# Grouping the activations of the gate, pointwise and feed-forward products by tile, with the side work held meanwhile

## The chip, the cores and the metric

The kernel runs on one core of one Trainium2 chip. The metric is device time in microseconds (us) of one execution; the kernel before is given as the median of three runs. TensorE is PE in the profile (its weight loads are PEld), VectorE is DVE, ScalarE is ACT, GpSimd is POOL and SyncE, which issues most of the DMAs, is SP.

## The reference

Two layers, all in float32, on an image batch of 4 x 64 x 64 positions with 256 channels.

```python
# layer 0, a block with a selective scan
xz = layernorm(x) @ in_proj_W                      # 256 -> 2 x 384
x_proj, z = split(xz)
y_ssm = 0.5 * (scan_fwd(windows(x_proj)) + scan_bwd(...))   # 2x2 windows, 8 states, dt = silu(...)
y_dw = depthwise_3x3(x_proj)
y_conv = gelu(y_dw @ pw_W)
y = (alpha * y_ssm + (1 - alpha) * y_conv) * silu(z) @ out_W
x1 = x + y
x1 = x1 + gelu(layernorm(x1) @ fuse_W1 + fuse_b1) @ fuse_W2 + fuse_b2   # 256 -> 512 -> 256
# layer 1, self-attention of each image over its 4096 positions
f, g, h = x1 @ Wf + bf, x1 @ Wg + bg, x1 @ Wh + bh  # 32, 32 and 256 channels
out = gamma * (softmax(g @ f.T) @ h @ Wo + bo) + x1
```

## The kernel before

Layer 0 is cut into 32 tiles of 512 positions (8 image rows; 8 tiles to an image, `NBLK` = 8). Layer 1 takes 128 queries at a time against 32 chunks of 128 keys; the last ones, when layer 0 is done, are taken 256 at a time by other functions (`late_weights`, `attend_late`).

The source is a set of Python generators. Each yields an estimated cost after every small piece of work, and the order in which the generators are advanced is the order in which instructions are written down. A scheduler then orders them for each engine, earlier written first where both are ready. What sets the written order:

- `scan(at)` is the chain of a tile. A step forms decays on ACT (`decays`, Exp, L406), transposes them on PE into a PSUM bank (`turned`, L462), and multiplies and adds on DVE (`decayed` L470 and L474, `carried` L492, `given` L485).
- Beside it run the side pieces of the tile before and of the next one: `conv` (the depthwise taps, on DVE from the second image on, L595), `gate` (three products with `win`, L342, each followed by a Silu, L346), `tail` (three pointwise products, L626, each with two Gelus, L631; the output product, L649; a layer norm; four feed-forward products, L669, each with a Gelu, L673; the second feed-forward product, L680; the inputs of layer 1) and `next_head` (layer norm and first product of a coming tile, L327). `weave` advances two of them in proportion to their costs. `first_layer` gives the side pieces 1.2 cost units for each unit of the scan (`SHARE`).
- `prepare(at)` makes what the next tile's scan needs, the steps `dt` among it (six products L382, six Silus L389), at the end of the scan before.
- From the second image on, layer 1 is the outer loop: `attend` writes eight steps of four value products (L1039) for 128 queries, and behind each step calls `fill(5.7)`, which advances layer 0 by 5.7 cost units (`RATE`). `weights` makes the scores (L844, copied out of PSUM by ACT in L852), their maxima (DVE, L860) and the exponentials (L877, L878) of the next queries.

PSUM has eight banks. Three are for the scan (`bank`), one is for the value products, and four (`q0` to `q3`) are handed out in turn by `aside()` to every side product; `four()` takes all four for a set of scores.

ACT holds one set of function tables at a time. Exp, Silu and Gelu are in different sets, so that a change from one to another puts an ACT_TABLE_LOAD before the instruction, whose time the profile puts down to that instruction's line. Copies and the Identity function need no load. For the tiles of the first image `gate` is already written as one run (`whole`); for the others each of its three products is a piece of its own:

```python
nc.scalar.activation(zs[:, f, :], pz, AF.Silu, bias=b_in[:, KI + f : KI + f + 1])
if not whole:
    yield 1.72
```

Of the kernel before, what the change touches and what calls it, by code (L numbers as in the profile page):

```python
# [31 lines left out]
NST = 8  # L32
# [27 lines left out]
def block_then_attention_kernel(  # L60
# [111 lines left out]
        return ins  # L172

    turn = [0]

    def aside(shape=(P, TOK)):

# [158 lines left out]
    def gate(at, whole):  # L336
        xnT = heads[at][0]
        zs = one.tile([P, KI, TOK], F32, tag="zs", name="zs")
        for f in range(KI):
            pz = aside()  # L340
            for k in range(KD):
                nc.tensor.matmul(  # L342
                    pz, lhsT=win[:, k, INNER + f * P : INNER + (f + 1) * P], rhs=xnT[:, k, :],
                    start=(k == 0), stop=(k == KD - 1),
                )
            nc.scalar.activation(zs[:, f, :], pz, AF.Silu, bias=b_in[:, KI + f : KI + f + 1])  # L346
            if not whole:
                yield 1.72
        gates[at] = zs
        if whole:  # L350
            yield 5.2

    def prepare(at):

        _, xc = heads[at]

        pj = aside()
        for k in range(KI):
            nc.tensor.matmul(pj, lhsT=wx[:, k, :], rhs=xc[:, k, :], start=(k == 0), stop=(k == KI - 1))
        proj = one.tile([P, TOK], F32, tag="proj", name="proj")  # L360
        nc.scalar.copy(proj, pj)
        yield 2.58
        pbc = aside((P, 4, 2, 64))
        for t in range(4):
            nc.tensor.transpose(pbc[:, t].rearrange("p d e -> p (d e)"), proj[:, t * P : (t + 1) * P], ident)
        bc = two.tile([P, 4, 2, 2 * NST], F32, tag="bc", name="bc")
        nc.vector.tensor_copy(bc, pbc[:, :, :, RANK:])
        cbn = st.tile([P, 8, NST], F32, tag="cbn", name="cbn")
        bc8 = bc.rearrange("p t d e -> p (t d) e")
        nc.vector.tensor_tensor(cbn, bc8[:, :, :NST], bc8[:, :, NST:], ALU.mult)  # L370
        cb = st.tile([P, 8], F32, tag="cb", name="cb")
        nc.vector.tensor_reduce(cb, cbn, AX.X, ALU.add)
        yield 1.1
        dts = [two.tile([P, KI, TOK], F32, tag="dt", name="dt") for _ in range(2)]
        for f in range(KI):
            pds = [aside() for _ in range(2)]

            with tc.high_priority():
                last = None
                for d in range(2):  # L380
                    last = behind(
                        nc.tensor.matmul(  # L382
                            pds[d], lhsT=wdt[64 * d : 64 * d + RANK, f * P : (f + 1) * P],
                            rhs=proj[64 * d : 64 * d + RANK, :], start=True, stop=True,
                        ),
                        last,
                    )
            for d in range(2):
                nc.scalar.activation(  # L389
                    dts[d][:, f, :], pds[d], AF.Silu, bias=v("dt_b_b" if d else "dt_b_f", f)  # L390
                )
            if at >= NBLK:
                yield 1.1
        steps[at] = bc, cb, dts, {}
        if at < NBLK:
            yield 3.3
            if at > 0:
                yield from gate(at - 1, True)
        decays(at, 0, 0)

    def decays(at, n, d):
# [25 lines left out]
    def scan(at, ensue):  # L427
# [69 lines left out]
        pas = {(0, 0): turned(0, 0)}  # L497
        for j in range(3 * NST + 1):
            n, k = divmod(j, 3)
            first, second = j < 3 * NST, j > 0  # L500
            if k == 2 and n + 1 < NST:
                decays(at, n + 1, 1)
            if first and k == 1 and n + 1 < NST:
                decays(at, n + 1, 0)
            p0 = decayed(0, j, pas.pop((0, j))) if first else None
            p1 = decayed(1, j - 1, pas.pop((1, j - 1))) if second else None
            if first:
                carried(0, j, p0)
                if j + 1 < 3 * NST:
                    pas[0, j + 1] = turned(0, j + 1)  # L510
                pas[1, j] = turned(1, j)
                yield 1.3
            if second:
                carried(1, j - 1, p1)
            if first:
                given(0, j, p0)
            if second:
                given(1, j - 1, p1)
            yield 2.0
            if j == 3 * NST - 4:  # L520
                ensue = ensue()
            if j >= 3 * NST - 4:
                for cost in ensue:
                    yield cost
                    if j < 3 * NST and cost > 2.0:
                        break
# [88 lines left out]
    def tail(at):  # L615
# [4 lines left out]
        load_rows(xo, at)  # L620

        yz = one.tile([P, KI, TOK], F32, tag="yz", name="yz")
        for f in range(KI):
            pw = aside()
            for k in range(KI):
                nc.tensor.matmul(  # L626
                    pw, lhsT=wpw[:, k, f * P : (f + 1) * P], rhs=ydw[:, k, :],
                    start=(k == 0), stop=(k == KI - 1),
                )
            for t2 in range(2):  # L630
                nc.scalar.activation(  # L631
                    yz[:, f, t2 * 256 : (t2 + 1) * 256].rearrange("p (t1 wr wc) -> p t1 wr wc", t1=2, wr=ROWS // 2),
                    pw.rearrange("p (wr t2 wc t1) -> p t2 t1 wr wc", wr=ROWS // 2, t2=2, t1=2)[:, t2],
                    AF.Gelu,
                )
            yield 2.58

        for f in range(KI):
            nc.vector.scalar_tensor_tensor(
# [23 lines left out]
        if at + 3 < LAST:  # L663
            load_head(at + 3)
        ff = one.tile([P, KF, TOK], F32, tag="ff", name="ff")
        for f in range(KF):
            pf = aside()
            for k in range(KD):
                nc.tensor.matmul(  # L669
                    pf, lhsT=wf1[:, k, f * P : (f + 1) * P], rhs=h2T[:, k, :],  # L670
                    start=(k == 0), stop=(k == KD - 1),
                )
            nc.scalar.activation(ff[:, f, :], pf, AF.Gelu, bias=b_f1[:, f : f + 1])  # L673
            yield 1.72
        for t2 in range(2):
            pq = aside((P, 2, DIM))
            for t1 in range(2):
# [50 lines left out]
    def weave(a, na, b, nb):  # L728

        da, db, ga, gb = 0.0, 0.0, True, True  # L730
        while ga or gb:
            if ga and (not gb or da * nb <= db * na):
                c = next(a, None)
                if c is None:
                    ga = False
                    continue
                da += c
            else:
                c = next(b, None)
                if c is None:  # L740
                    gb = False
                    continue
                db += c
            yield c

    def first_layer():
        beside = []

        def more():

            while beside:
                cost = next(beside[0], None)
                if cost is not None:
                    return cost
                beside.pop(0)
            return None

        def drain(what, at):
            while ready[what] < at:
                cost = more()  # L760
                if cost is None:
                    break
                yield cost

        yield from head(0)
        load_head(1)
        diagonals()
        yield from prepare(0)
        for at in range(LAST):
            beside.append(side(at))  # L770

            def ensue():
                if at + 1 < LAST:
                    yield from drain("head", at + 1)
                    yield from prepare(at + 1)

            credit = 0.0
            for cost in scan(at, ensue):
                yield cost
                credit += SHARE * cost  # L780
                while credit > 0.0:
                    cost = more()
                    if cost is None:
                        break
                    credit -= cost
                    yield cost
            yield from drain("halo", at)
            if at + 1 < LAST:
                yield from inputs(at + 1, 0)
            yield from merge(at)  # L790
        yield from drain("tail", LAST - 2)
        yield from conv(LAST - 1)
        yield from gate(LAST - 1, False)
        yield from tail(LAST - 1)
        ready["tail"] = LAST - 1

# [86 lines left out]
    def fill(us):  # L883

        debt[0] += us
        while debt[0] > 0:
            cost = next(layer, None)
            if cost is None:
                debt[0] = 0.0
                break  # L890
            debt[0] -= cost
# [298 lines left out]
```

## Time and profile before

| | before |
|---|---|
| median of 3 runs | 5246.53 us (5246.45 to 5246.89) |
| span of the profiled execution | 5245.1 us |
| PE busy | 4861.3 us (93%) |
| DVE busy | 4585.4 us (87%) |
| ACT busy | 3582.8 us (68%) |
| ACT_TABLE_LOAD | 653 of 1283 ns |
| mean granted TensorE clock | 0.972 |

The time of the profiled execution is that of its span and of 1.4 us that the median of the runs has over it. The span has three stretches: tiles without attention (the first scores start at 866 us), tiles with attention between them (the last product of a tile starts at 4622 us), and attention alone. A group of the profile is one line of the source on one engine with its count, its busy time, the mean time of one instruction, and the idle time of the engine just before these instructions with what ended it. A busy engine is not the bound by that alone: where two engines take turns in leading, the idle time of each is cover for the other.

### The profile page before, as it was taken

The numbers are of one execution on the slowest core, as the hardware profiler recorded it, in microseconds if no ns is written. First come the engines' busy times: TensorE is split into PE (matmuls) and PEld (weight loads), VectorE is DVE, ScalarE is ACT, GpSimd is POOL, SyncE is SP. The second block draws the span as 40 slices with busy tenths as digits, with TensorE's granted clock in tenths as the row PEclk, the third lists the DMA queues.
The fourth block names the chain that finished last, engine by engine and source line by source line (L and its number), as shares of the span: only waits on it lengthen the run. The fifth ranks groups of instructions, "written<-read, shape, count | busy, mean of one in ns | idle before, by whom it ended". The sixth has DMA issues, their size and how long they took to land. (4 is left out here: it accounts for less than half of the span.)

```text
span 5245.1 us, 77394 instructions
## 1 busy us (share of the span) xinstructions
PE 4861.3 (93%) x27444; PEld 3509.2 (67%) x27444; DVE 4585.4 (87%) x8391; ACT 3582.8 (68%) x5508; POOL 208.3 (4%) x304
## 2 busy tenths in 40 slices
PE   7999998899999999999899999999999889899999
PEld 4565565666666666666666666666666666678887
DVE  7999999889989989988999988899889898866665
ACT  6778778667776767766676766777676767455554
POOL 0000000000000000000000000000000000000000
PEclk8999999999999999999999999999999999999999
DMA  1010011344444434444434444444444344344444
GB/s 48 26 44 19 23 34 36 119 127 126 135 128 135 129 122 122 131 127 124 134 119 127 131 124 127 122 134 128 130 131 131 115 129 130 121 146 147 148 146 139
DMA packets 355779, 592.13 MB, mean 113 GB/s; under 512 B 55104, under 2 KB 95296, under 8 KB 355392
## 3 DMA queue, kind: packets, MB, share of 16 engines
q1 hardware_dynamic: 351872, 583.31, 36.7%
q8 instruction: 217, 3.56, 0.3%
q10 hardware_dynamic: 3520, 3.87, 0.2%
q14 instruction: 170, 1.39, 0.1%
HBM read 528.18 MB, written 58.79 MB: 112 GB/s over the span
## 5 line engine op out<-in xcount | busy, mean ns | idle before, releaser
L1039 PE MATMUL acc<-vt,eq 128*128 128x257 f32 x5888 | 1521.2, 394 | 41.3 <-issue 19.3
L1039 PEld LDWEIGHTS acc<-vt,eq 128*128 128x128 f32 x5888 | 1090.2, 196 | 296.9 <-issue 130.7
L406 ACT ACTIVATE e<-dt,a_sc 128x384 f32<-128x384 f32 x1536 | 853.0, 611 | 250.0 <-PE bank L462 239.7
L462 PE MATMUL bank<-ident,e 128*128 128x128 f32 x4320 | 662.1, 280 | 105.9 <-DVE p L474 59.1
L462 PEld LDWEIGHTS bank<-ident,e 128*128 128x128 f32 x4320 | 523.4, 143 | 329.4 <-issue 94.3
L492 DVE SCALAR_TENSOR_TENSOR h<-u,bc,p 128x384 f32<-128x384 f32 x1024 | 613.1, 611 | 0.1
L852 ACT COPY eq<-q 128x512 f32<-128x512 f32 x736 | 386.1, 588 | 306.7 <-PE q L844 191.4
L485 DVE SCALAR_TENSOR_TENSOR y<-h,bc,y 128x384 f32<-128x384 f32 x960 | 589.4, 614 | 3.6 <-ACT y L483 1.3
L474 DVE TENSOR_TENSOR p<-bank,h 128x384 f32<-128x384 f32 x960 | 515.5, 547 | 49.1 <-PE bank L462 48.4
L878 ACT ACTIVATE eq<-eq 128x1024 f32<-128x1024 f32 x368 | 383.2, 1052 | 145.1 <-DVE eq L877 142.7
L877 DVE TENSOR_TENSOR eq<-eq,nb 128x1024 f32<-128x1024 f32 x368 | 443.6, 1217 | 23.0 <-ACT nb L873 22.6
L595 DVE SCALAR_TENSOR_TENSOR ydw<-xp,vec,ydw 128x512 f32<-128x512 f32 x640 | 462.8, 742 | 0.4
L1014 PE MATMUL bank<-vt,eT 128*128 128x257 f32 x1728 | 432.3, 382 | 0.0
L860 DVE TENSOR_TENSOR mx<-mx,eq 128x512 f32<-128x512 f32 x552 | 382.5, 693 | 52.7 <-ACT eq L852 45.2
L1014 PEld LDWEIGHTS bank<-vt,eT 128*128 128x128 f32 x1728 | 323.4, 189 | 55.6 <-issue 8.6
L485 DVE SCALAR_TENSOR_TENSOR y<-p,bc,y 128x384 f32<-128x384 f32 x512 | 314.0, 613 | 0.1
L626 PE MATMUL q<-ydw,wpw 128*128 128x512 f32 x576 | 282.8, 625 | 30.9 <-ACT eq L852 18.1
L470 DVE SCALAR_TENSOR_TENSOR p<-bank,bc,u 128x384 f32<-128x384 f32 x480 | 291.5, 607 | 17.4 <-PE bank L462 17.0
L406 ACT ACT_TABLE_LOAD x225 | 288.7, 1283 | 10.8 <-PE bank L462 7.0
L844 PE MATMUL q<-gq,fQ 32*128 32x128 f32 x5888 | 246.8, 293 | 35.5 <-ACT eq L852 17.5
L844 PEld LDWEIGHTS q<-gq,fQ 32*128 32x128 f32 x5888 | 202.6, 194 | 105.4 <-ACT eq L852 26.9
L948 DVE TENSOR_TENSOR mx<-mx,eT 128x512 f32<-128x512 f32 x252 | 174.4, 692 | 95.5 <-ACT eT L943 74.8
(153 smaller groups left out, 7021.0 us busy)
## 6 DMA issues: line engine op xcount, KB each, us to landing
vt<-vod SPq DMA_DIRECT2D x1760, 257.0 KB, 2.8
vod<-vst SPq DMA_DIRECT2D x32, 514.0 KB, 4.1
xt<-in_x_dram SPq DMA_DIRECT2D x256, 64.0 KB, 1.9
xo<-in_x_dram SPq DMA_DIRECT2D x256, 64.0 KB, 2.6
x1d<-xo SPq DMA_DIRECT2D x32, 512.0 KB, 2.9
res<-x1d SPq DMA_DIRECT2D x92, 128.0 KB, 2.8
out_dram<-res SPq DMA_DIRECT2D x368, 32.0 KB, 1.6
fgd<-fg SPq DMA_DIRECT2D x32, 256.0 KB, 2.1
```

What stands on the lines that cost most here:

```text
L406: nc.scalar.activation(e[:, f, :], dts[d][:, f, lo : lo + 3 * P], AF.Exp, scale=a_sc[:, d, f * NST + n : f * NST + n + 1],)
L462: nc.tensor.transpose(pa[:, f * P : (f + 1) * P], es[d, n][:, f, off : off + P], ident)
L474: nc.vector.tensor_tensor(p, pa[:, :INNER], hs[d], ALU.mult)
L485: nc.vector.scalar_tensor_tensor(y[:, t, :], h, c, y[:, t, :], ALU.mult, ALU.add)
L492: nc.vector.scalar_tensor_tensor(hs[d], u[d][:, t, :], bc[:, t, d, n : n + 1], p, ALU.mult, ALU.add)
L595: nc.vector.scalar_tensor_tensor(o, x_tap, w_tap, o, ALU.mult, ALU.add)
L844: ins = nc.tensor.matmul(pr[r][:, s * P : (s + 1) * P], lhsT=fQ[CK * r : CK * (r + 1), at : at + P], rhs=gq[CK * r : CK * (r + 1), :], sta ...
L852: nc.scalar.copy(e[:, j, :], pr[2 * a + j])
L877: nc.vector.tensor_tensor(e8, e8, nb.unsqueeze(1).broadcast_to([P, 8, P]), ALU.add)
L878: nc.scalar.activation(e, e, AF.Exp)
L1014: nc.tensor.matmul(sums[c][:, : DIM + 1], lhsT=e[:, r % 2, s, c * P : (c + 1) * P], rhs=vt[:, s, :], start=(n == 0 and s == 0), stop=(n == ...
L1039: nc.tensor.matmul(acc[:, : DIM + 1], lhsT=es[k // 2][:, k % 2, a : a + P], rhs=vt[:, s, :], start=(n == 0 and s == 0), stop=(n == 2 * NI ...
```

## The change

In `gate`, in the pointwise part of `tail` and in its feed-forward part, all products of the tile are written first, each into its own bank, and then all activations. While a set is open, a flag `held` makes `weave` stay with the same generator, makes `fill` go on past its debt until the set is closed, and, in the last four steps of a scan (`ending`), makes `first_layer` go on with side pieces past their credit. `prepare` yields its cost for the steps once, not after each of the three pairs of products, for all tiles.

```diff
     def gate(at, whole):
         xnT = heads[at][0]
         zs = one.tile([P, KI, TOK], F32, tag="zs", name="zs")
+        pzs = []
         for f in range(KI):
             pz = aside()
...
-            nc.scalar.activation(zs[:, f, :], pz, AF.Silu, bias=b_in[:, KI + f : KI + f + 1])
-            if not whole:
+            pzs.append(pz)
+            if not whole and f + 1 < KI:
+                held[0] = True
                 yield 1.72
+        for f in range(KI):
+            nc.scalar.activation(zs[:, f, :], pzs[f], AF.Silu, bias=b_in[:, KI + f : KI + f + 1])
+        held[0] = False
         gates[at] = zs
-        if whole:
-            yield 5.2
+        yield 5.2 if whole else 1.72
...
     def prepare(at):
...
-            if at >= NBLK:
-                yield 1.1
         steps[at] = bc, cb, dts, {}
-        if at < NBLK:
-            yield 3.3
-            if at > 0:
-                yield from gate(at - 1, True)
+        yield 3.3
+        if 0 < at < NBLK:
+            yield from gate(at - 1, True)
         decays(at, 0, 0)
...
         for j in range(3 * NST + 1):
             n, k = divmod(j, 3)
+            ending[0] = j >= 3 * NST - 4
...
     def tail(at):
...
+        pws = []
         for f in range(KI):
             pw = aside()
...
+            pws.append(pw)
+            if f + 1 < KI:
+                held[0] = True
+                yield 2.58
+        for f in range(KI):
             for t2 in range(2):
                 nc.scalar.activation(
                     yz[:, f, t2 * 256 : (t2 + 1) * 256].rearrange("p (t1 wr wc) -> p t1 wr wc", t1=2, wr=ROWS // 2),
-                    pw.rearrange("p (wr t2 wc t1) -> p t2 t1 wr wc", wr=ROWS // 2, t2=2, t1=2)[:, t2],
+                    pws[f].rearrange("p (wr t2 wc t1) -> p t2 t1 wr wc", wr=ROWS // 2, t2=2, t1=2)[:, t2],
                     AF.Gelu,
                 )
-            yield 2.58
+        held[0] = False
+        yield 2.58
...
+        pfs = []
         for f in range(KF):
             pf = aside()
...
-            nc.scalar.activation(ff[:, f, :], pf, AF.Gelu, bias=b_f1[:, f : f + 1])
-            yield 1.72
+            pfs.append(pf)
+            if f + 1 < KF:
+                held[0] = True
+                yield 1.72
+        for f in range(KF):
+            nc.scalar.activation(ff[:, f, :], pfs[f], AF.Gelu, bias=b_f1[:, f : f + 1])
+        held[0] = False
+        yield 1.72
...
     def weave(a, na, b, nb):
         da, db, ga, gb = 0.0, 0.0, True, True
+        first = True
         while ga or gb:
-            if ga and (not gb or da * nb <= db * na):
+            if not held[0]:
+                first = ga and (not gb or da * nb <= db * na)
+            if first:
...
             for cost in scan(at, ensue):
                 yield cost
                 credit += SHARE * cost
-                while credit > 0.0:
+                while credit > 0.0 or (held[0] and ending[0]):
...
     def fill(us):
         debt[0] += us
-        while debt[0] > 0:
+        while debt[0] > 0 or held[0]:
```

More of the change, by code (lines that the diff above doesn't have):

```diff
@@ L174, in block_then_attention_kernel @@
     turn = [0]
+    held = [False]
+    ending = [False]
     def aside(shape=(P, TOK)):
```

## The prediction

> **What bounds the kernel now.** First the page's busy times and slices, to see which engine could be the bound.
>
> ```profile
> PE 4861.3 (93%) x27444; PEld 3509.2 (67%) x27444; DVE 4585.4 (87%) x8391; ACT 3582.8 (68%) x5508; POOL 208.3 (4%) x304
> ...
> PE   7999998899999999999899999999999889899999
> ...
> DVE  7999999889989989988999988899889898866665
> ACT  6778778667776767766676766777676767455554
> ```
>
> PE and DVE are both at nine tenths until the layer ends (slice 35); ACT, which the change relieves, is at seven. The slices are too coarse to say who leads, so the next view is the busy time in the three stretches of one tile (1294 to 1453 us), which begins with the Gelu of its feed-forward part. The columns are the stretch, its length, then PE, PEld, DVE, ACT and POOL busy, the clock and the DMA.
>
> ```profile
> 1294.00:1336.00 42.00, 41.89 (x245) 31.54 (x244) 31.78 (x63) 30.92 (x44) 1.37 (x3) 1.00 0.46 140
> 1336.00:1424.00 88.00, 82.61 (x482) 59.30 (x480) 87.78 (x154) 73.94 (x111) 0.00 (x0) 0.98 0.44 133
> 1424.00:1453.00 29.00, 24.75 (x171) 17.78 (x169) 26.64 (x52) 16.29 (x26) 4.85 (x6) 1.00 0.38 119
> ```
>
> The feed-forward stretch is PE's (41.89 of 42 us), the one with gate, taps and pointwise products is DVE's (87.78 of 88), and in the short third, with layer norm and output product, neither is full. The same cut through 21 tiles gives means of 42.88 us of PE in 44, 80.01 of DVE in 82, and 28.30 of DVE in 31. What the leader leaves idle is 1.12 + 1.99 + 2.70 = 5.8 us a tile, 134 us over the 23 tiles of this kind: the ceiling for a gain that keeps this order of stretches.
>
> Then the groups of table loads, whose count the change is about, and PE's waits between 1049 and 4458 us (engine, line, what it waited for, us in total, times, longest).
>
> ```profile
> L406 ACT ACT_TABLE_LOAD x225 | 288.7, 1283 | 10.8 <-PE bank L462 7.0
> L878 ACT ACT_TABLE_LOAD x99 | 127.0, 1283 | 2.3 <-DVE eq L877 0.6
> L631 ACT ACT_TABLE_LOAD x89 | 114.2, 1283 | 31.7 <-PE q L626 14.9 <-issue 14.3 <-DMA vt<-vod 1.6
> L673 ACT ACT_TABLE_LOAD x86 | 110.3, 1283 | 1.5
> L346 ACT ACT_TABLE_LOAD x80 | 102.6, 1283 | 1.4
> L389 ACT ACT_TABLE_LOAD x72 | 92.4, 1283 | 1.3
> ```
>
> ```profile
> PE bank L462 <- DVE p L474: 35.3, 33, 3.2
> PE bank L462 <- DVE p L470: 34.9, 26, 2.9
> ...
> PE q L626 <- ACT eq L852: 18.1, 15, 2.2
> ...
> PE q L844 <- ACT eq L852: 15.9, 10, 2.6
> ...
> PE q L669 <- ACT eq L852: 4.4, 4, 2.0
> PE q L844 <- ACT zs L346: 4.2, 7, 1.6
> ...
> PE q L844 <- ACT yz L631: 2.5, 6, 0.7
> ...
> PE q L844 <- ACT ff L673: 2.1, 3, 1.3
> ```
>
> ACT ends 94 of PE's some 250 us of waits there, mostly as the engine that has not yet copied a set of scores out of the four side banks; DVE ends more. In DVE's own list ACT ends 110 us. So ACT is in the way at times, not the bound.
>
> **Part 1: fewer table loads.** In the order of the changed program, which can be built without being run, ACT has 460 loads for 653: Exp of the decays 153 for 225, of the attention 76 for 99, pointwise Gelu 56 for 89, feed-forward Gelu 56 for 86, gate 47 for 80, steps 70 for 72. The sets are not perfectly closed; the scheduler still puts an Exp into many of them. That is 193 x 1.283 = 248 us of ACT, 22 loads in the first eight tiles and 171 of 510, a third, in the tiles with attention. On the path counts only what makes the leader of a stretch wait for ACT. Summed over the 21 tiles, ACT ended 15.5 us of PE's waits in the first stretch, 16.9 of DVE's in the second, 9.6 of DVE's in the third: 42, or 46 us for 23 tiles. A third off is 16 us. That is the low end; the high end is a third of all 204 us that PE and DVE waited for ACT, 69 us. I take 35, near the middle, because the engine that doesn't lead is at nine tenths as well and its delays come back soon after. Below nothing this part can't go: it only takes work away. In the first eight tiles DVE waited for ACT for about 5 us in all; I take 1.
>
> The Trainium skill, "ScalarE: Activation LUTs", section "Table sets: the hidden batching unit", says to batch activations by table set and puts a switch at about 2.7 us. This trace has 1283 ns for every load, so the page's price would make 521 us of ACT from the 193 loads, and the trace's 248 us stands.
>
> **Part 2: products that stood behind a set of scores.** Before, scores come between the products of a set (56 times in 23 tiles in the written-out PE order), and the next product waits for ACT to empty a bank. After, none do. Only the feed-forward ones lie where PE leads: 4.4 us, of which a third is counted already. I take 3 more.
>
> **Part 3: banks held until the set closes.** A set now fills three or, in the feed-forward part, all four side banks, and scores need all four. In PE's order over 23 tiles, scores begin within 2 us of PE work behind the last product of a set 4 times before and 14 times after. Then PE's queue stands at the scores, with value products and decay transposes behind them, and behind those DVE's `p` and the maxima. Price: 0.55 us each from the trace (zs, yz and ff rows: 8.8 us in 16 waits), up to a load and four Gelus, 1.283 + 4 x 0.687 = 4.0 us. Ten more are 5 to 40 us. I take one load each, 13 us, since the scheduler lets the first activation start when its product is there. It can't be below nothing.
>
> The Trainium skill, "Perfetto Trace Analysis", section "Optimizing Tensor Performance", Matmuls, speaks against this part: independent groups should rotate through the banks so that emptying one overlaps the next group's products. Taken at its word, each of 69 sets would show two activations that it hid, 69 x 2 x 0.687 = 95 us slower, against the 13 us above; the rows of waiting scores, 8.8 us in all, are nearer to the latter.
>
> **Part 4: side products in lumps.** In PE's order the work from first to last product shrinks from 25.6 to 8.4 us for the gate, 20.3 to 11.6 pointwise, 15.4 to 8.6 feed-forward, with 1 to 3 us of other work inside. The danger is that the scan's transposes stop meanwhile and DVE, the leader of the second stretch, runs dry. But over the whole tile the places where more than 8 us of PE work lie between neighbouring groups of transposes are 80 before and 88 after, of 1104. So I take 0. If the cover (DVE's taps, maxima and adds) failed, the excess of two lumps a tile over that 8 us, (8.4 - 8) + (11.6 - 8) = 4 us, times 23 is 92 us slower. If grouping leaves more DVE work for later holes it can be below nothing, within the 134 us ceiling.
>
> Costing nothing: the single yield in `prepare` (70 loads for 72, same instructions); SP's queue, whose loads and stores keep their number, with five value buffers in hand and 3.0 us of weight-load waits for them in the trace; POOL, at 4%. The stretch of attention alone is the same program.
>
> **Sum.** 5245.1 - 35 - 1 - 3 + 13 + 0 = 5219; with the 1.4 us that the median of the runs lies above the profiled span, about 5221 us, 0.5% faster.
>
> **Rivals.** *No change.* The leaders are PE and DVE, and the relief falls on the third engine: the low end of part 1 (16 + 1 + 3) against 13 gives 5240 us. For it: DVE at 97.6% in the long stretch. Against: ACT at 82% there (67.1 of 82 us), where waits build up.
> *Slower.* The held banks decide: 69 sets end with ACT still to work, and late scores make late copies, maxima and exponentials. At 4 us for 14 to 20 such places, half of the 92 us of lumps and 20 us of relief: 56 + 46 - 20 = 82 at the worst, about 35 at the middle, 5280 us. It decides once the price of a held bank passes 3.9 us for ten places, or 1 us for each of 40 (scores within 4 us behind a set are 20 before, 42 after). For it: the four-bank sets sit in PE's own stretch.
> *Larger gain.* The 69 us of part 1 come in full and some of the idle 134 with them: 5160 us. For it: all three engines are above 80% in the long stretch. Against: its DVE is at 97.6% already.
> *The change not doing what it says* is excluded by the order: 193 loads do go.
>
> **How the numbers follow.** Chances: forecast 0.40, larger gain 0.09, no change 0.17, slower 0.34. About 0.2% (10 us) is what a measurement of this kernel can tell from none. So faster 0.49, same 0.17, slower 0.34. The range of 8 in 10 runs from 5165, which leaves out most of the larger gain, to 5285, which leaves out the worse half of the slower case, 82 us. It holds both signs; the forecast's own range is 5190 to 5236.
>
> **What would show it.** Right: 460 loads of 1283 ns; ACT busy down by some 248 us to 3335; PE's waits for `eq` at L626 and L669 (new lines) near gone; DVE in the second stretch still over 97%; PE idle down by about 25 us. Wrong: scores waiting for zs, yz and ff for far more than 22 us; waits of `p` for its bank on DVE well above 48 us, which would be the lumps; idle time of the leader unchanged, which would be the second case. A change of the granted clock in the tiles would be outside this sum.

## The result, and the profile after

The changed kernel takes 5267.11 us (median of five runs, 5262.41 to 5271.04) against 5246.53 us: a ratio of 1.0039, 95% interval 1.0027 to 1.0051. It is slower by 20.6 us where the forecast was faster by 25.5 us. The profiled execution has a span of 5269.3 us, 24.2 us over that of before; it is the slowest of the five, 3.9 us above their median. Busy times and slices of the page:

```profile
PE 4884.7 (93%) x27444; PEld 3527.4 (67%) x27444; DVE 4593.6 (87%) x8391; ACT 3331.0 (63%) x5315; POOL 206.6 (4%) x304
...
PE   7999998899999988999999999999999889899999
...
DVE  7999999999999999888998888999899998866665
ACT  6667766666666576665667666766665666445554
```

ACT has shed 252 us and the kernel is none the faster: PE's busy time rose by 23 us for the same 27444 products. The loads went as the built order said:

```profile
L409 ACT ACT_TABLE_LOAD x153 | 196.3, 1283 | 5.4 <-PE bank L465 2.9
...
L641 ACT ACT_TABLE_LOAD x56 | 71.8, 1283 | 22.9 <-issue 12.1 <-PE q L631 9.2 <-PE bank L465 1.1
L690 ACT ACT_TABLE_LOAD x56 | 71.8, 1283 | 0.9
...
L354 ACT ACT_TABLE_LOAD x47 | 60.3, 1283 | 0.7
```

Since a few microseconds decide, the first step is to cut the span at the first scores and at the first value product of the stretch of attention alone, in both profiled executions:

| stretch | before | after | difference | forecast |
|---|---|---|---|---|
| up to the first scores | 866.1 | 905.2 | +39.1 | -1 |
| tiles with attention | 3777.6 | 3760.9 | -16.7 | -25 |
| attention alone | 601.5 | 603.2 | +1.7 | 0 |

The whole loss lies in the first image, where the forecast saw nothing. The windows there, from 130 us to the first scores, before and then after (columns as in the prediction: length, PE, PEld, DVE, ACT and POOL busy, clock, DMA):

```profile
130.00:866.00 736.00, 698.91 (x3046) 433.56 (x3044) 717.68 (x1451) 571.26 (x908) 49.90 (x74) 0.99 0.09 28
```

```profile
130.00:905.00 775.00, 714.05 (x3043) 443.17 (x3041) 723.96 (x1457) 540.65 (x885) 50.82 (x76) 0.96 0.08 27
```

Before, DVE leads this stretch at 97.5%; after, no engine is full. PE's busy time is 15 us longer and its granted clock 0.96 for 0.99, so part of the loss is clock and the rest is idle time. PE's and DVE's waits from 100 to 900 us name what they waited for; first PE and DVE before, then PE after, then DVE after:

```profile
PE q L312 <- DVE h L303: 12.5, 15, 1.5
```

```profile
DVE xt L303 <- POOL rstd L301: 1.2, 1, 1.2
...
DVE p L470 <- PE bank L462: 0.3, 1, 0.3
```

```profile
PE q L314 <- DVE h L305: 28.0, 14, 3.6
PE q L660 <- DVE yz L653: 13.1, 16, 1.8
```

```profile
DVE p L473 <- PE bank L465: 17.0, 14, 2.8
DVE xt L305 <- POOL rstd L303: 11.8, 8, 1.5
```

PE stands for `h`, the layer norm ahead of the feed-forward part, up to 3.6 us at a time for 1.5 before; DVE stands 17.0 us for the scan's transposed decays (`p`), which was 0.3 us before, and 11.8 us in its own next layer norm for 1.2. PE's second row, 13.1 us for `yz` where before had 3.1, belongs to the pointwise set, and run 2 below keeps it (15.3 us) without the loss. The timeline of one such place (start, length, engine, line, operation, and in brackets the idle time before it), first before, then after:

```profile
448.26 1.98 PE L327 MATMUL q<-xnT,win 128*128 128x512 f32 x4
...
451.78 0.41 PE L312 MATMUL q<-ident,h 128*128 128x128 f32 x2 [1.54 <-DVE h L303]
...
452.03 1.02 PE L327 MATMUL q<-xnT,win 128*128 128x512 f32 x2
...
453.98 1.02 PE L327 MATMUL q<-xnT,win 128*128 128x512 f32 x2
```

```profile
466.18 0.67 PE L314 MATMUL q<-ident,h 128*128 128x128 f32 x4 [3.65 <-DVE h L305]
...
469.03 2.07 PE L681 MATMUL q<-h2T,wf 128*128 128x512 f32 x2 [0.46 <-ACT h2T L315]
...
476.63 3.60 PE L681 MATMUL q<-h2T,wf 128*128 128x512 f32 x8
...
480.06 1.88 PE L329 MATMUL q<-xnT,win 128*128 128x512 f32 x4
...
482.31 0.62 DVE L473 SCALAR_TENSOR_TENSOR p<-bank,bc,u 128x384 f32<-128x384 f32 x1 [2.75 <-PE bank L465]
```

Three things are to be seen. PE stands idle for 3.65 us. The first two products after the transposes of `h` take 2.07 us, and a pair of the same form took 1.02 us at the same place before: the granted clock is 0.5 from 467.8 us on, for 6.8 us. Then eight feed-forward products and four of `next_head` (L329) come with no decay transpose between them, and DVE runs dry for 2.75 us. Before, `next_head`'s product of 1.98 us lies in the wait for `h`, which leaves a gap of 1.54 us, and the next one, in two halves of 1.02 us, lies among the transposes of `h` and right behind them. In seven of the eight tiles before, 8 of the 12 matrix instructions of `next_head` stand between the output product and the transposes of `h`, 2 among the transposes and 2 right behind; in all eight after, 4 stand ahead of the transposes and 8 behind the 16 of the feed-forward set. That is the work of `held` in `weave`: while a set is open it stays with `tail` and does not advance `next_head`.

In the tiles with attention, the same tile as in the prediction, cut at the same pieces of work (first feed-forward Gelu, last value product of `tail`, first `xo` of the output product):

```profile
1332.00:1374.00 42.00, 41.89 (x244) 31.51 (x243) 31.76 (x64) 25.80 (x40) 1.37 (x3) 1.00 0.45 140
1374.00:1461.00 87.00, 81.06 (x477) 58.30 (x475) 86.80 (x151) 66.43 (x105) 0.00 (x0) 0.98 0.44 135
1461.00:1490.00 29.00, 24.98 (x169) 17.92 (x170) 27.89 (x57) 16.06 (x26) 4.57 (x6) 1.00 0.34 103
```

In this tile PE still fills the first stretch and DVE the second; ACT has fallen from 73.94 to 66.43 us in the second and it became 1 us shorter. PE's waits there (1049 to 4478 us):

```profile
PE q L865 <- ACT eq L873: 41.9, 24, 2.6
PE bank L465 <- DVE p L473: 35.4, 24, 2.9
PE bank L465 <- DVE p L477: 34.2, 32, 2.2
...
PE q L865 <- ACT yz L641: 2.5, 3, 1.1
PE q L865 <- ACT zs L354: 2.2, 5, 0.8
...
PE q L681 <- ACT eq L873: 0.8, 1, 0.8
```

The pointwise products no longer wait for `eq` (18.1 us before, no row now). But a set of scores now waits for the copies of the set before it: 41.9 us for 15.9. Over all lines PE waited 68.3 us for `eq` before and 64.0 after: the wait has changed its place and little more. In the traces, the PE work between one group of scores and the next is under 2 us 19 times (before: 13) and under 6 us 29 times (before: 18), of 183.

### The profile page after: what moved, and what is told of

Its sections match the earlier page's. It is cut to its first block, busy times and chain, and to the rows that moved or that the text cites. A ratio compares the mean times of both kernels' runs of the same rounds, so it can differ in the third digit from the quotient of the medians.

```text
span 5269.3 us, 77144 instructions
## 1 busy us (share of the span) xinstructions
PE 4884.7 (93%) x27444; PEld 3527.4 (67%) x27444; DVE 4593.6 (87%) x8391; ACT 3331.0 (63%) x5315; POOL 206.6 (4%) x304
## 4 chain that ended last, share of the span: by engine, by line
PE 45%; DVE 27%; ACT 9%; issue 3%; POOL 1%; DMA 1%; DVEq 0%; SPq 0%; POOLq 0%; ACTq 0%
PE acc L1060 12%; PE bank L1035 7%; DVE y L488 4%; DVE ydw L599 4%; DVE eq L898 3%; PE bank L465 3%; PE q L698 3%; DVE mx L881 3%; DVE h L495 3%; PE q L681 3%; DVE p L477 3%; PE acc L1035 3%; PE q L865 2%; PE q L329 2%; PE q L956 1%
## 5 line engine op out<-in xcount | busy, mean ns | idle before, releaser
L1060 PE MATMUL acc<-vt,eq 128*128 128x257 f32 x5888 | 1518.5, 394 | 41.9 <-DVE res L1005 26.5
L865 PE MATMUL q<-gq,fQ 32*128 32x128 f32 x5888 | 270.7, 296 | 58.8 <-ACT eq L873 42.8
L865 PEld LDWEIGHTS q<-gq,fQ 32*128 32x128 f32 x5888 | 217.9, 195 | 141.3 <-ACT eq L873 60.7
L631 PE MATMUL q<-ydw,wpw 128*128 128x512 f32 x576 | 268.8, 601 | 6.5 <-DVE ydw L599 6.5
L681 PE MATMUL q<-h2T,wf 128*128 128x512 f32 x512 | 251.7, 631 | 4.9 <-ACT h2T L315 3.6
```

The costliest lines, as they stand in the source:

```text
L681: nc.tensor.matmul(pf, lhsT=wf1[:, k, f * P : (f + 1) * P], rhs=h2T[:, k, :], start=(k == 0), stop=(k == KD - 1),)
L865: ins = nc.tensor.matmul(pr[r][:, s * P : (s + 1) * P], lhsT=fQ[CK * r : CK * (r + 1), at : at + P], rhs=gq[CK * r : CK * (r + 1), :], sta ...
L1060: nc.tensor.matmul(acc[:, : DIM + 1], lhsT=es[k // 2][:, k % 2, a : a + P], rhs=vt[:, s, :], start=(n == 0 and s == 0), stop=(n == 2 * NI ...
```

## The experiments

Theory: `held` and the lumps moved `next_head` and the scan's transposes off their places in the first image, which costs idle time and clock. Rival: the held banks or the loads themselves decide. Each ratio is against the kernel before on the same chip, with its 95% interval; "first scores" is the length of the first stretch, "the rest" the profiled span less that, 4379.0 us before and 4364.1 after, and "half clock" the time from 130 us to the first scores in which the profile shows a granted clock of 0.5: 10.2 us before, 61.4 after.

**1. Both of `tail`'s sets undone in the first image.** For tiles with `at < NBLK` the pointwise and feed-forward activations follow their products as before; the rest is the changed kernel.

```diff
             pfs.append(pf)
-            if f + 1 < KF:
+            if not (at >= NBLK):
+                nc.scalar.activation(ff[:, f, :], pf, AF.Gelu, bias=b_f1[:, f : f + 1])
+                yield 1.72
+            elif f + 1 < KF:
                 held[0] = True
                 yield 1.72
```

> In the tiles of the first image the pointwise and feed-forward activations stand behind each product again; all other tiles as after. Theory (hold in weave): of the 39 us that the first scores came later all come back and the 16 us that the tiles with attention won stay: about 5230 us, 0.3% under before; first scores near 866 us; TensorE at half clock for about 10 us before them, not 61. Rival (the loss is spread, the 16 us are noise of two runs): about 5246.

Measured: 5234.32 us, 0.9979 (0.9970 to 0.9988); first scores at 864.0 us, PE idle from 100 us on 38.1 us for 61.2 in the changed kernel. The loss is in the sets of the first image.

**2. Only the feed-forward set undone there** (the diff above alone), **3. only the pointwise set undone there** (the same edit at `pws`).

> In the first image only the feed-forward set is undone, the pointwise set stays. Theory (the open feed-forward set keeps weave with the tail, so that two of the next head's three products, which stood in the layer norm's gap on PE, fall behind the set): nearly all comes back, 5228 to 5234 us, PE gaps over 3.5 us gone before the first scores. Rival (late pointwise Gelus make the tail's chain late): about 5260.

> In the first image only the pointwise set is undone, the feed-forward set stays. Theory: nothing comes back of the layer norm's gap, 5260 to 5268 us, the seven PE gaps over 3.5 us and some 60 us at half clock stay. Rival (late pointwise Gelus): 5230 to 5240.

Measured: without the feed-forward set 5231.37 us, 0.9967 (0.9954 to 0.9979), first scores at 865.2; without the pointwise set 5277.86 us, 1.0058 (1.0046 to 1.0071), first scores at 903.8. The loss up to the first scores is the feed-forward set's, the pointwise set has no part in it.

**4. The converse: the kernel before with the feed-forward set in the first image alone** (648 loads).

```diff
+            pfs.append(pf)
+            if not (at < NBLK):
+                nc.scalar.activation(ff[:, f, :], pf, AF.Gelu, bias=b_f1[:, f : f + 1])
+                yield 1.72
+            elif f + 1 < KF:
+                held[0] = True
+                yield 1.72
```

> The kernel before with one part of the change alone: the feed-forward set, in the tiles of the first image only. Theory (the open set holds the next head's products out of the layer norm's gap): the first scores come some 35 to 40 us later, 5280 to 5290 us, seven PE gaps over 3.4 us and some 60 us at half clock before them. Rival (it takes the other sets of the change as well): 5246 to 5255.

Measured: 5281.6 us, 1.0068 (1.0056 to 1.0081); first scores at 901.8, half clock 61.4 us as in the changed kernel. One set in eight tiles makes 36 of the 39 us.

**5. `next_head` sooner.** All sets stay; in the first image `weave` gives `next_head` a larger share, first 22 cost units, and later 18 instead.

```diff
-        yield from weave(tail(at - 1), 46.0, next_head(at), 14.0)
+        yield from weave(tail(at - 1), 46.0, next_head(at), 18.0 if at <= NBLK else 14.0)
```

> All sets as after; in the tiles of the first image weave gives the next head's pieces a larger share (22 for 14), so that its products come before the feed-forward set opens. Theory: they are in the layer norm's gap again though the set stays, the gaps over 3.5 us and most of the half clock go: 5230 to 5245 us. Rival (the set itself, its late Gelus or its lump on PE, makes DVE run dry): no change against after, 5262 to 5270.

> All sets as after; weave's share for the next head in the first image is 18 (14 in after, 22 in the run with the head earlier), at which the written PE order has two whole products of the next head between the output product and the transposes of the layer norm, and two more only behind the whole feed-forward set. Theory (gap and half clock): gaps of 3.4 us gone, half clock before the first scores from 61 to about 10 us, first scores near 870 us, total 5230 to 5240. Rival (the four-product lump lets DVE run dry whatever lies in the gap): first scores at 890 or later, 5255 or more.

Measured with 22: 5266.98 us, 1.0037 (1.0024 to 1.0049), first scores at 894.4. This run missed its theory: the products came for the most part ahead of the gap, not into it, and PE still stands for `h`, 23.5 us in 8 waits. With 18 more of them falls into it: 5245.14 us, 1.0000 (0.9991 to 1.0008), first scores at 874.4, half clock 34.1 us. Its window up to there:

```profile
130.00:874.00 744.00, 709.95 (x3044) 436.27 (x3043) 716.03 (x1450) 542.58 (x887) 47.97 (x74) 0.98 0.09 28
```

From the first statistics of the layer norm to the first transpose of `h` some 4 us pass in all these kernels. In most tiles `next_head` gives PE 2.47 us of work in that time before, none after, 0.96 with 22 and 1.94 with 18, and PE is idle for 1.66, 3.64, 2.77 and 2.15 us of it. With every set kept and the loads as few, 31 of the 39 us are back with 18. So in the first image it is where `next_head` falls, not the held banks.

**6. Clock or idle time?** Dummy products into `spare`, a side bank, while the layer norm is awaited: six of 8 columns, and in another kernel two of 512 columns.

```diff
+        if spare is not None:
+            for k in range(2):
+                nc.tensor.matmul(
+                    spare[:8, :], lhsT=mv.rearrange("p t e -> p (t e)"), rhs=wf1[:, k % 2, :],
+                    start=(k == 0), stop=(k == 1),
+                )
...
-        layernorm(h2, xo)
+        layernorm(h2, xo, aside() if at < NBLK else None)
```

> The changed kernel with six small products without use that can run only in the layer norm's gap (they read its statistics), in the tiles of the first image; PE's order is otherwise the same. It adds work and leaves the place of the next head's products as it is. Theory (about half of the 39 us is the half clock that follows a gap over 3.4 us): no gap over 3.4 us, time at half clock before the first scores from 61 to some 10 us, first scores 15 to 25 us earlier than in after, 5242 to 5254 us. Rival (the order alone, with DVE waiting behind the lump): no change or slower, 5265 to 5275.

> The changed kernel with two products without use in the layer norm's gap of the first image, as in the run with the gap kept busy, but 512 columns wide instead of 8, so that TensorE streams through the gap. If half clock follows from how little PE does in the gap: time at half clock before the first scores from 61 to about 10 us, first scores 10 to 25 us earlier than in after (905), as the clock alone is worth that. If the half clock is only a sign and the order costs the time: first scores within 5 us of 905.

Measured: 8 columns, 5275.91 us, 1.0056 (1.0044 to 1.0069), which misses the theory: no gap over 2.5 us is left, yet half clock is 58.0 us for 61.4 and the first scores start at 905.4. 512 columns, 5262.37 us, 1.0034 (1.0022 to 1.0045): half clock 20.5 us, first scores at 895.0, and DVE still idle for 45 us from 100 us on, for 55 in the changed kernel (before: 22). Its window:

```profile
130.00:895.00 765.00, 716.54 (x3077) 439.50 (x3074) 724.79 (x1457) 540.73 (x885) 50.84 (x76) 0.99 0.09 27
```

The clock is back at 0.99 and 10 of the 39 us with it. That doesn't make the other 29 the order's alone. The first kernel of run 5 is the opposite case: half clock stays (64.9 us), while DVE's wait for the lump's `p` falls from 17.0 to 1.5 us, and it has 11 us back. The kernel with 18, which mends both in part, has 31 back, more than the 10 and the 11 together: the 39 us can't be split into a share of the clock and one of the order. The spare bank is taken from the four in turn, so that every later side product has another bank; what that does was not separated.

**7. What are the loads worth?** Before and after with Exp in place of Silu, Gelu and Sigmoid, which leaves one load. The order of the instructions does not stay quite the same: up to the first scores another instruction stands in 482 of some 3440 places of PE's order and 237 of 904 of ACT's, in the kernel before; but `next_head` and the transposes of `h` lie as they did in each kernel. These two compute other functions there. ACT's busy time of 2750.7 us in the first is that of before less 652 loads within 5 us, so Exp itself costs the same.

```diff
-                    AF.Gelu,
+                    AF.Exp,
```

> The kernel before with Exp in place of Silu, Gelu and Sigmoid, so that one table load is left of 653; the output is not the reference's. It prices all loads. By the prediction's part 1 (35 us for a third of the loads in the tiles) some 105 us less, 5140 us; by its low end (16 us for a third) 5195 us; if ACT never leads, no change.

> The changed kernel with Exp in place of Silu, Gelu and Sigmoid; output not the reference's. Beside the kernel before without switches it shows what the order of the change costs when no load is left to save: theory, the 39 us of the first image stay and the banks held in the other tiles cost 0 to 15 us, so 35 to 55 us over the kernel before without switches. Rival (the order itself is neutral): within 10 us of it.

Measured: before without loads 5203.93 us, 0.9917 (0.9904 to 0.9931); after without loads 5273.49 us, 1.0051 (1.0038 to 1.0063). So 652 loads, 837 us of ACT, together with the order that comes with them, are worth 42 us in the kernel before, 0.06 us each, where the prediction's 35 us would have made it 105 and its low end 50; the 459 in the kernel after show no worth. With one load left in either, the order of the change costs 38 us up to the first scores (911.9 against 874.3) and 38 us in the rest (4366.3 against 4327.9). These are single profiled executions, and that of the second kernel is the slowest of its five: by the medians the two together are 70 us, not 76, more than the 35 to 55 that were expected. The first 38 us show that the loss of the first image needs no loads; the second hold for this pair alone.

**8. Single sets in the tiles with attention.** The gate set, the feed-forward set, the pointwise set, and the last two together, each with the other sets undone everywhere as in 1. The gate set comes with the single yield of `prepare`; the other three have the yields of before.

```diff
-            pzs.append(pz)
-            if not whole and f + 1 < KI:
-                held[0] = True
+            nc.scalar.activation(zs[:, f, :], pz, AF.Silu, bias=b_in[:, KI + f : KI + f + 1])
+            if not whole:
                 yield 1.72
```

> Of the change only the gate's set (and the single yield of the steps), which touches the tiles with attention alone; 578 loads. All 653 loads were worth 42 us in the kernel before, so 75 are worth about 5. Theory (a set costs banks and order as well): 5236 to 5246 us. Rival (grouping is free): 5238 or less with no new wait of the scores.

> Of the change only the feed-forward set, in the tiles with attention alone; 597 loads, 56 fewer. It takes all four side banks in PE's own stretch. Theory (held banks cost where PE leads): no gain, 5245 to 5258 us. Rival (its switches are worth their share, 4 us, and the bank costs nothing): 5238 to 5243.

> Only the pointwise set is kept, in the tiles with attention alone; 605 loads instead of 653. The feed-forward set by itself was worth 15 us for 56 loads, the gate set nothing for 75. Theory (a set pays where PE leads its stretch, since there its products close up and DVE has work in hand; it costs where DVE leads): the pointwise set lies in DVE's stretch, so no gain, 5243 to 5256 us, PE's waits of scores for eq as before (16 us). Rival (it is the number of loads that counts, the gate set was spoilt by its scores): 48 loads at the whole kernel's price of 42/653 us each are 3 us; with the feed-forward's price, 0.27 us a load, 13 us: 5233 us.

> Pointwise and feed-forward sets, in the tiles with attention alone; 549 loads. If the two act independently the gain is the sum of the two runs of one set: 15 us of the feed-forward set, plus what the pointwise set alone shows beside it. Theory: 5228 to 5236 us, no better than the feed-forward set alone. Rival (with the gate's set the pointwise one also brings its gain, and it is the gate that spoils the tiles with attention): 5218 us, the best version so far.

The last two columns are PE's waits for `eq` from 1049 to 4458 us, at the scores and at the pointwise products.

| sets kept | loads | us | ratio | scores | pointwise |
|---|---|---|---|---|---|
| none (before) | 653 | 5246.53 | 1 | 15.9 | 18.1 |
| gate | 578 | 5247.94 | 1.0010 (1.0001 to 1.0019) | 27.7 | 16.2 |
| feed-forward | 597 | 5230.28 | 0.9973 (0.9962 to 0.9984) | 16.0 | 17.0 |
| pointwise | 605 | 5239.70 | 0.9992 (0.9983 to 1.0000) | 28.8 | 5.1 |
| pointwise and feed-forward | 549 | 5246.77 | 1.0002 (0.9993 to 1.0011) | 28.8 | 4.5 |

With the pointwise set the waits of its own products are 13.0 us less and those of the scores 12.9 us more; the gate set adds 11.8 us at the scores; the feed-forward set leaves both alone. But the feed-forward set gains more than its theory and its rival allowed, and the times do not add up: against the runs of before on the same chips, -13 (feed-forward) and -5 us (pointwise) alone, +2 together. Neither the theory nor the rival of the last run foresaw that.

**9. How much does any shift of the order move?** The kernel before with `RATE` 5.65 and 5.75 for 5.7. Nothing is grouped.

```diff
-RATE = 5.7
+RATE = 5.65
```

> The kernel before with RATE 5.65 for 5.7: the same instructions, only the points at which side work falls between value products shift a little; no set is grouped. The single sets did not add up (feed-forward -13 us, pointwise -4, gate +5, pointwise and feed-forward together +2). Theory (any shift of the written order moves the tiles with attention by about 10 us in either direction, so single sets' times hold no more than that): the stretch from the first scores to the late value products differs from the kernel before's 3778 us by 4 to 15 us, either sign. Rival (the order of before is not that touchy, and the sets' differences are their own): within 3 us, 5242 to 5248 us.

> The kernel before with RATE 5.75 for 5.7, the other direction. Theory: as for 5.65, 4 to 15 us away from before, the sign not the mirror image of the other. Rival: within 3 us of 5245 us, or a smooth effect of the rate, with opposite signs in the two runs.

Measured: 5255.19 us, 1.0014 (1.0005 to 1.0022), and 5232.23 us, 0.9973 (0.9961 to 0.9985). Up to the first scores nothing changes (864.6 and 865.0 us), the rest takes 4387.5 and 4354.6 us, the second in the fastest of its twelve executions. By the medians the two are 8 us above and 15 us under before: a 1% change of one constant moves the tiles with attention by as much as a set does. PE's waits for `eq` at the pointwise products fall to 11.9 and 10.0 us without any set, too; at the scores they stay (15.2 and 13.7). The two signs are opposite, so a smooth effect of the rate isn't excluded; two points don't tell. Either way, what a single set gains or loses there can't be told from the shift that it makes. The best times, 5230.28 us (feed-forward set alone) and 5231.37 us (no such set in the first image), are some 0.3% under before, and no proof that grouping as such is worth that much.

## Why the prediction was wrong

**What held.** The 460 loads, ACT at 3331.0 us for a forecast 3335, the end of the waits for `eq` at the pointwise products, DVE over 97% in the second stretch of the tile (86.80 of 87). PE's idle time in the tiles with attention fell from 309.3 to 285.8 us, 24 for a forecast 25, but that is luck: only 5 us of it are waits that ACT ended, and over the whole kernel PE's idle time stayed (383.8 to 384.6). DVE's longest row for `p` there went from 48.4 to 51.7 us only, so the lumps did little in those tiles.

**The step that failed: the first eight tiles, costed at -1 us.** Part 1 looked at them only for waits that ACT ends, and parts 3 and 4 counted places in the order over the 23 tiles with attention alone. The set of the feed-forward part moves `next_head`, and no step costed what `held` in `weave` passes by. The cover that it took away was named nowhere: `next_head`'s products fill the time in which the layer norm goes through DVE and POOL. In the tiles with attention value products lie there too, 9.5 us of PE on the average; in the first image the decay transposes give 0.6 us and nothing else does. The order that was at hand showed it: all of `next_head`'s products stand ahead of the set before, and two thirds of them behind it after. Its price was +39.1 us: 24 us more idle PE (37.4 to 61.2 from 100 us on) and 15 us of longer products. Runs 1 to 4 show that the feed-forward set alone does it, run 5 that `next_head`'s place is worth 31 us of it, clock and all, and run 6 that mending the clock alone brings 10; how the rest divides was not shown.

**Parts 1 and 2, together -38 in the tiles with attention.** Their estimate went by waits: a third of the loads gone, so a share of the 204 us that PE and DVE waited for ACT. That step failed. From 1049 us to near the end of those tiles ACT ended 93.9 us of PE's waits and 109.8 of DVE's before, 88.9 and 106.9 after: 8 us less, not 35. (The thirds in the prediction come to 15 and 68 us, not 16 and 69, and the 5 us for which DVE waits for ACT in the first eight tiles reach to 1000 us, 3.1 to the first scores; nothing rests on either.) Even without any load 54.0 and 94.0 are left, so three quarters of those waits are put down to ACT's place in the chain (a copy that comes when its scores come), not to loads. What the loads are worth does not show in those waits alone: without any, that stretch and the end take 4327.9 us, 51 less than before, though in another order; and the 460 loads that are left show no cost behind the new order (4366.3 without them, 4364.1 with them). For the whole kernel the load is a small thing: 42 us are 5% of its ACT time.

**Part 3, +13, and part 4, 0:** too small by the pair without loads, +38 for the whole new order. That -51 + 38 comes near the -15 us that this stretch and the end gained is no further evidence: with the -2 from 4366.3 to 4364.1 it is the same difference taken in three steps. The waits that were to show part 3, scores for `zs`, `yz` and `ff`, came to 4.7 us and not over 22. A price was paid in another place: 26 us more of scores waiting for `eq` of the scores before. The likely reason is that `fill` runs on until a set closes and then has a debt to work off, so that value steps and both score groups follow closely; that the gate and the pointwise set each bring 12 to 13 us of these waits supports it, and so does the pair without loads, where the same row goes from 1.8 to 21.3 us; but the lull itself was not varied. Part 4's bound, the excess of lumps over 8 us, was drawn for tiles with attention; the lump that cost something, DVE's 17.0 us for `p`, lies in the first image.

**The size of the gain there stays uncertain.** Eight kernels keep all sets in the tiles with attention (after, runs 1 to 3, both of 5 and both of 6); their rest is 4363 to 4375 us, 4369 in the mean. The two with none there (before and run 4) have 4379.0 and 4375.2. That makes some 8 us gained, not 15, of the 25 forecast, and 11 if the medians of all runs are taken for the profiled spans, at a scatter of the same size.

**The rivals.** The slower case came in, with less than its middle time and by another mechanism. Held banks did not make the loss of the first image: run 5 keeps all of them, and 31 of the 39 us are gone. What part they have in the 38 us of run 7 in the tiles with attention was not separated from the rest of the order. The prediction's price at which they decide over 40 places counts those of before in; over the 22 new ones it is 1.8 us and not 1. The Trainium skill, "Perfetto Trace Analysis", "Optimizing Tensor Performance", says that independent groups should rotate through the banks, and the prediction reads from it 95 us for the 69 sets; the 38 us of run 7 stay well below that.

**The clock** had been left outside the sum, and it was in it. The Trainium skill, "TensorE: Matmul & The Clock Gate", Part 1, says that an idle window of about 3.4 us puts PE back to half clock and that activity restores it. The trace agrees for the changed kernel: at each of the seven gaps of 3.64 us a stretch of 6.8 us at half clock begins, at most 2 us from the gap's end. It does not agree for shorter gaps, as the last section shows, and there the measurement decides.

## What to carry to other kernels

Before a lock or a flag goes into a scheduler, list every generator that it holds back and look what those pieces cover, in each phase of the program and not only in the long one: eight tiles of 32 lost more here than the other 24 gained. A table load saved on an engine that does not lead is worth what it makes the leader wait, here some 0.06 of 1.28 us, and a new order can cost as much as all of them. Where a 1% change of a planner's constant moves the time by 0.1 to 0.3%, a gain of that size needs several neighbouring orders before it is put down to the edit.

## What the runs showed of the hardware

Instructions alone did not keep the clock up: with six products of 8 columns in the gap, half clock stayed at 58.0 us; with two of 512 columns it fell to 20.5 us. From 130 us to the first scores the stretches at half clock come in lengths of 3.4, 6.8 and 10.2 us, and their starts in the first image of the changed kernel lie 99.0 or 102.4 us apart, multiples of 3.41 us, as if a fixed window were judged and not a gap. Gaps under 3.4 us are enough at times: in the kernel before a gap of 2.3 us at 818 us was followed by 3.4 us at half clock, in the first kernel of run 5 eight waits of mostly 2.8 us went with 64.9 us at half clock, and in the second, with no gap over 1.8 us, half clock was 34.1 us.

The spread between executions of one program goes with the granted clock: twelve of the kernel with `RATE` 5.75 had spans from 5219.6 us at a mean clock of 0.977 to 5246.7 us at 0.970. A single profiled span of this kernel is therefore worth some 10 us either way.
